# A tenth place for weights, base rows stored block by block, and edits to the routing of a two-layer graph network

## The chip, the cores and the metric

The kernel runs on one core of a Trainium2 chip, all in float32. The metric is the device time of one execution in microseconds (us); lower is better. A core has a matrix engine (TensorE, "PE" in the profile; its weight loads are "PEld"), three engines for elementwise work (VectorE "DVE", ScalarE "ACT", GpSimd "POOL"), and SyncE ("SP"), which here only issues transfers. Each engine works through its own queue in order. Transfers (DMA) can be issued from SP, ACT and POOL, and share sixteen DMA engines. "Granted clock" is the share of its full clock that TensorE was given.

## The reference, cut to what matters

Two layers run over 384 nodes of 1024 features. Each layer is graph attention, plus a mixing attention, plus a mixture of eight experts. All three parts are added to the nodes.

```python
xn = layernorm(x)
x = x + L0_gnn(xn, edges) + L0_mix(xn)      # layer 0: attention with a mask from the edges
x = x + L0_ffn(layernorm(x))                # top 2 of 8 experts: silu(a) * g, 1024 -> 352 -> 1024
xn = layernorm(x)
x = x + L1_gnn(xn, src, dst) + L1_mix(xn)   # layer 1: edge weights exp(-leaky_relu(al + ar))
x = x + L1_ffn(layernorm(x))                # top 1 of 8 experts

def L0_ffn(h):                  # the routing of layer 0
    q, k, v = split(h @ wqkv.T, 3)                       # 8 columns each
    logits = einsum(softmax(q[..., None] * k[..., None, :]), v)
    top, idx = top_k(logits, 2); scores = softmax(top)
    ...
def L1_ffn(feats):              # the routing and the experts of layer 1
    aff = feats @ centroids.T; eid = argmax(aff); alpha = sigmoid(aff[eid])
    h = layernorm(feats) * gamma[eid] + beta[eid]
    y = feats + relu(h @ w1[eid] + b1[eid]) @ w2[eid] + b2[eid]
    return alpha * y + (1 - alpha) * feats               # feats + alpha * (relu(..) @ w2 + b2)
```

## The kernel before, in words

The nodes lie in `x` as three blocks of 128 rows (index `nb`). A block is turned to "features by nodes" with eight 128x128 transposes on TensorE (`to_t`, L211): the first four are copied out of PSUM by VectorE, the others by ScalarE. `norm_on_both` (L200) normalises the first half of a block on VectorE and the second on ScalarE.

**Weights.** Every weight is a load of up to 2 MB issued by SP into a "place" of 16 KB per partition (`load_w`, L117). `ring` (L101) is a list of pools: `next_w` (L103) takes the first entry and puts it at the end, so places are used in turn. A place is free once the matmuls that read its last weight are done. There are nine places in the end: three in `wpool`, one `w_top` (L609), two `w_more` (L730), and three `w_last` (L1158), which become usable when layer 1's middle tiles are closed (`mid.close()`, L1156).

**Order.** A planner (the Tile framework) orders each engine's queue beforehand by program order and its own estimate of what is ready. An engine then waits at the head of its queue, whatever stands behind. `tc.issue_after(i)` keeps instructions behind `i` on the engine of `i`. `held` (L301) makes a transfer wait until another instruction, or the transfer it issues, is done. A pool opened in memory that earlier pools have used waits for the release of them all; with `reuse_waits="tile"` each tile waits only for the tiles it overlaps.

**Layer 0's routing** (L753 to L799). For each block, `to_router` multiplies by `wqkv`, takes the statistics and normalises, and `ready(AF.Exp, ..)` reads one element through ScalarE to bring its table in. `to_places` (L767) runs `route_block` (L351: some twenty small VectorE steps around one Exp, and again a `ready`), ranks the nodes with small matmuls (`place_both`, L383), and scatters the rows to their expert's places in DRAM (`xg0`). `to_first` (L773) gathers the rows of expert 0 by a matmul with one-hot columns into the PSUM tiles `first`. `sums` (L787) adds up the centroids' rows by eight matmuls with a matrix of ones, `csum` is its copy; `too_many` (L341) counts whether an expert got more than its places.

**Layer 0's experts** (`experts0_sorted`, L891). Expert 0 uses `keep["xe0"]`; the others load 128 rows from `xg0` (L905) and transpose them (L910), then `hidden_of` (L914), `by_feature`, and the second matmuls (L972). Results go to DRAM, and nodes gather their two rows back (`take`, L994; the last half as `take_back`, L988).

**Layer 1** (`layer1`, L1021). Block by block: gather (`take_back`), add, normalise, transpose (L1054), multiply by `w_gnn` in two halves (L1058). Then keys, the graph part, values, queries, and `w_fc` (`project`, L1161). `to_router` (L1190) mixes a block (`mix_norm`, which is the last reader of `gamma`), takes the affinities, and makes both the experts' input `xb` and the base rows in `x` (`add_normed`, L187: feats plus the residual). `to_places` scatters `xb` to `xg`, and `info` (gate and node number) to `ig`.

**Layer 1's experts** (`experts1_sorted`, L1336). Pairs of experts share one 128-row tile. For each pair: `rows_of` (transposes and `scaled`), `hidden_of` (L1371), `by_feature` (transposes, ReLU, `hT`), `give` (L1394: second matmuls L1402, times the gate L1405, then a scatter that adds to `out` in DRAM). Biases are gathered for each node (L1412), added to the base rows (L1421), and these are stored by SP (L1423) before the first scatter may add to them.

Of the kernel before, what the change touches and what calls it, by code (L numbers as in the profile page):

```python
# [10 lines left out]
F32 = mybir.dt.float32  # L11
# [6 lines left out]
P = 128  # L18
# [27 lines left out]
def gps_two_layers(ctx: ExitStack, tc: tile.TileContext, d, out: bass.AP):  # L46
# [153 lines left out]
    def norm_on_both(dst, src, mean, rinv):  # L200

        off = small.tile([P, 1], F32, tag="off", name="off")
        ve.tensor_scalar(off, mean, rinv, -1.0, op0=OP.mult, op1=OP.mult)
        first = ve.tensor_scalar(dst[:, :HB], src[:, :HB], mean, rinv, op0=OP.subtract, op1=OP.mult)
        ac.activation(dst[:, HB:D], src[:, HB:D], AF.Identity, bias=off, scale=rinv)
        return off, first
# [134 lines left out]
    def too_many(pool, tag, oh, cap):  # L341
        ps = pool.tile([P, HB], F32, tag=tag, name="total")
        for b in range(NB):
            mm(ps[:, :X], lhsT=ones_q, rhs=oh[:, b, :], start=b == 0, stop=b == NB - 1)
        most = small.tile([P, 1], F32, tag="pl_m", name="pl_m")
        ve.tensor_reduce(most, ps[:, :X], AX.X, OP.max)
# [4 lines left out]
    def route_block(ps, sums, off, rinv, apart):  # L351
# [6 lines left out]
        qk = small.tile([P, X, X], F32, tag="r_qk", name="r_qk", bufs=1)  # L358
# [5 lines left out]
        ready(AF.Sqrt, qk[:, 0, 0:1])  # L364
# [3 lines left out]
        ve.tensor_tensor(qk, qk, qkv[:, 2, None, :].to_broadcast([P, X, X]), OP.mult)  # L368
        logit = small.tile([P, X], F32, tag="r_l", name="r_l")
        ve.tensor_reduce(logit, qk, AX.X, OP.add)  # L370
# [45 lines left out]
    with ExitStack() as layer:  # L416
# [6 lines left out]
        with tc.tile_pool(name="edges", bufs=1) as ed, tc.tile_pool(name="hot", bufs=2) as hot, \  # L423
# [17 lines left out]
            for kc in range(KC):  # L441
                mm(ps[:, :3 * X], lhsT=ones_q, rhs=wr[:, kc, :], start=kc == 0, stop=kc == KC - 1)
# [6 lines left out]
            with tc.issue_after(copied[0].ins):  # L449
                ve.tensor_copy(wsum, ps[:, :3 * X])  # L450
# [283 lines left out]
        def row(cols, name, dtype=F32):  # L734
# [3 lines left out]
                "slot": row([NB], "slot4", I32), "own_e": row([NB], "own_e4", I32), "info": row([NB, 2], "info4"),  # L738
# [4 lines left out]
        with tc.tile_pool(name="ps_m0", bufs=4, space=PSUM) as pm, \  # L743
# [11 lines left out]
            def to_router(nb):  # L755
# [7 lines left out]
                off, _ = norm_on_both(xn[:, nb, :], x[:, nb, :], mean, rinv)  # L763
# [3 lines left out]
            def to_places(nb):  # L767
                oh = route_block(*queries[nb], share[:, 1, nb:nb + 1])
# [4 lines left out]
            def to_first(nb):  # L773
                for kc in range(KC):
                    mm(first[kc // 4][:, kc % 4, :], lhsT=xn[:, nb, kc * P:(kc + 1) * P], rhs=own0[:, nb, :],
                       start=nb == 0 and kc % 4 == 0, stop=nb == NB - 1 and kc % 4 == 3)
# [11 lines left out]
            for kc in range(KC):  # L788
                mm(ps[:, :X], lhsT=ones_q, rhs=cen[:, kc, :], start=kc == 0, stop=kc == KC - 1)
            to_places(NB - 1)  # L790
            to_first(NB - 1)
            ve.tensor_copy(keep["xe0"][0], first[0])
# [5 lines left out]
            ve.tensor_copy(csum, ps[:, :X])  # L798
            over0 = too_many(px, "x", both, CAP0)  # L799
# [91 lines left out]
    def experts0_sorted(keep):  # L891

        slots, share = keep["slots"], keep["share"]
        with tc.tile_pool(name="act6", bufs=1) as act, \
                tc.tile_pool(name="work6", bufs=2) as work, \
                tc.tile_pool(name="ps_h6", bufs=5, space=PSUM) as ph, \
                tc.tile_pool(name="ps_t6", bufs=3, space=PSUM) as pt:
# [88 lines left out]
            take_back(work.tile([P, D], F32, tag="xs", name="yt1").rearrange("p (a b) -> p a b", b=HB), 0)  # L986
# [34 lines left out]
    def layer1(keep=None):  # L1021


        with tc.tile_pool(name="act2", bufs=1) as act, \
                tc.tile_pool(name="work3", bufs=2) as work, \
                tc.tile_pool(name="ps_m2", bufs=4, space=PSUM) as pm, \
                tc.tile_pool(name="ps_x2", bufs=4, space=PSUM) as px:
            mid = ExitStack()
# [3 lines left out]
            xnT = act.tile([P, KC, N], F32, tag="byf", name="xnT2")  # L1032
# [3 lines left out]
            ws = [load_w(d["w_gnn"][hf]) for hf in range(2)]  # L1036
            taken, backs = None, []
# [5 lines left out]
            for nb in range(NB):  # L1043
                with ExitStack() as behind:
                    if nb:
                        behind.enter_context(tc.issue_after(normed_half.ins))
# [6 lines left out]
                    _, normed_half = norm_on_both(xn1[:, nb, :], x[:, nb, :], mean, rinv)  # L1053
                to_t(pm, xnT, xn1[:, nb, :], nb)  # L1054
# [25 lines left out]
            gamma, beta = act.tile([P, D], F32, name="gamma"), part.tile([P, D], F32, name="beta")  # L1080
# [57 lines left out]
            oT = act.tile([P, KC, N], F32, tag="byf", name="oT2")  # L1138
# [39 lines left out]
            if keep is None:  # L1178
                for nb in range(NB):
                    for hf in range(2):  # L1180
                        project(nb, hf)
                    mix_norm(nb)
                return
# [4 lines left out]
            sums, last = {}, []  # L1188

            def to_router(nb):  # L1190
                mix_norm(nb)
                xs, xb = x[:, nb, :], xn1[:, nb, :]
# [17 lines left out]
                norm_on_both(xb, xs, mean, again)  # L1210
                add_normed(xs, mean, rinv)
                sums[nb] = (ps, less, rinv)

            def to_places(nb):
# [7 lines left out]
                c = first_of(oh[:, nb, :], near, top)  # L1222
# [6 lines left out]
                ve.tensor_scalar(keep["own_e"][:, nb:nb + 1], c, -1.0, float(X), op0=OP.mult, op1=OP.add)  # L1229
                last[:] = [scatter(xg[:, :], [slot[:, nb:nb + 1]], [xb], X * CAP)]  # L1230

# [7 lines left out]
            for nb in range(1, NB):  # L1239
                project(nb, 0)  # L1240
                to_router(nb - 1)
                project(nb, 1)
                to_places(nb - 1)
# [5 lines left out]
            for g in range(2):  # L1249
                scaled(keep["xe0"][g], first[g], g, (0, 1))  # L1250
            at = [slot[:, nb:nb + 1] for nb in range(NB)]

            info = keep["info"]
            ac.activation(info[:, :, 0], most, AF.Sigmoid)
# [81 lines left out]
    def experts1_sorted(xe0):  # L1336

        with tc.tile_pool(name="act4", bufs=1) as act, \
# [6 lines left out]
            b2s = []  # L1345

            def load_rows(pair):
                xs = work.tile([P, D], F32, tag="row", name="xs4", bufs=4)
                gp.dma_start(xs, xg[pair * P:(pair + 1) * P, :])
                return xs  # L1350
# [190 lines left out]
```

## Time and profile before

| what | value |
|---|---|
| median of 3 runs | 1060.62 us (1059.91 to 1061.09) |
| the profiled execution | 1058.17 us, its span 1056.4 us |
| mean granted clock | 0.986 |
| bytes read from / written to HBM | 160.22 / 22.44 MB, 173 GB/s over the span |
| longest matmul group | L135, 512 matmuls, 165.7 us busy |
| last matmul ends | 1047.5 us |
| last output scatter issued / landed | 1048.56 / 1053.34 us |

The span is the time from the first to the last instruction; the run has 1.8 us around it. In a timeline row stand start, duration, engine, line, operation, output<-inputs, shapes, and in brackets the idle time of the engine before it and what ended it. "PE y L1402 <- SPq L1439: 2.4, 1, 2.4" reads: before the matmuls of L1402 TensorE waited 2.4 us in all, once, at most 2.4 at a time, for something released on SP's queue; a wait for a landed load shows so. In a row of windows stand the stretch, its length, busy us (and instructions), the granted clock, the share of time in which the DMA engines were busy, and GB/s. "Landing" is when a transfer's last byte has arrived.

### The profile page before, as it was taken

How to read it: one execution, taken by the hardware profiler on the slowest of the kernel's cores; microseconds unless marked ns; L12 is line 12 of the kernel's file. 1: busy time of each engine (PE TensorE's matmuls, PEld its weight loads, DVE VectorE, ACT ScalarE, POOL GpSimd, SP SyncE). 2: the span in 40 equal slices, each digit the busy share in tenths (PEclk: the TensorE clock that was granted, in tenths of full speed). 3: DMA queues.
4: the chain of work that ended last, by engine and by line, in shares of the span. 5: the costliest groups of instructions: out<-in, count | busy, mean ns of one | idle time of the engine just before them, and what ended most of it. 6: DMA issues, size and time to landing. Idle time of an engine off the chain costs nothing. (4 is left out here: it accounts for less than half of the span.)

```text
span 1056.4 us, 9529 instructions
## 1 busy us (share of the span) xinstructions
PE 1019.2 (96%) x3455; PEld 554.2 (52%) x3455; DVE 356.2 (34%) x993; ACT 270.6 (26%) x501; POOL 320.3 (30%) x277
## 2 busy tenths in 40 slices
PE   6999999999999999999998999989999999999995
PEld 5555555554455555544456666434444465656341
DVE  4580000007666766721333111043304100365321
ACT  3111111100776666621112101221212110113210
POOL 2142456566686678510001000050001100001231
PEclk9999999999999999999998999999999999998998
DMA  9939522424424342523155887969622222625994
GB/s 352 398 134 367 156 80 89 151 96 109 80 0 91 71 80 0 160 80 130 61 199 215 306 309 281 373 219 370 228 80 79 80 80 79 241 92 206 309 373 117
DMA packets 69525, 182.83 MB, mean 173 GB/s; under 512 B 21488, under 2 KB 22352, under 8 KB 69216
## 3 DMA queue, kind: packets, MB, share of 16 engines
q1 hardware_dynamic: 41072, 147.58, 38.6%
q0 software_dynamic: 25408, 29.93, 12.3%
q10 hardware_dynamic: 2992, 4.65, 1.2%
q8 instruction: 29, 0.48, 0.2%
q14 instruction: 24, 0.20, 0.1%
HBM read 160.22 MB, written 22.44 MB: 173 GB/s over the span
## 5 line engine op out<-in xcount | busy, mean ns | idle before, releaser
L482 POOL DMA_INDIRECT countd<-seen,cells x96 | 153.4, 1598 | 62.9 <-DMA countd<-seen,cells 37.7
L135 PE MATMUL mm<-xnT,w 128*128 128x384 f32 x512 | 165.7, 486 | 0.1
L135 PEld LDWEIGHTS mm<-xnT,w 128*128 128x128 f32 x512 | 97.1, 190 | 67.7 <-DVE xnT L219 0.4
L668 PE MATMUL mm<-xnT,w 128*128 128x384 f32 x384 | 132.4, 493 | 0.0
L482 POOL DMA_INDIRECT lastd<-typ,cells x96 | 96.7, 1007 | 108.4 <-DMA lastd<-typ,cells 70.9
L668 PEld LDWEIGHTS mm<-xnT,w 128*128 128x128 f32 x384 | 70.5, 190 | 56.4 <-issue 13.4
L716 PE MATMUL mm<-w,t 128*128 128x512 f32 x192 | 84.3, 595 | 0.8 <-DVE x L404 0.8
L147 PE MATMUL mm<-w,xnT 128*128 128x512 f32 x192 | 82.8, 592 | 0.0
L135 PE MATMUL mm<-t,w 128*128 128x384 f32 x256 | 82.7, 486 | 0.0
L919 PE MATMUL h<-w,xeT 128*128 128x352 f32 x224 | 68.5, 462 | 0.7 <-DVE xeT L911 0.4
L135 PEld LDWEIGHTS mm<-t,w 128*128 128x128 f32 x256 | 48.6, 190 | 33.9
L147 PEld LDWEIGHTS mm<-w,xnT 128*128 128x128 f32 x192 | 36.3, 190 | 45.5 <-issue 45.5
L716 PEld LDWEIGHTS mm<-w,t 128*128 128x128 f32 x192 | 35.9, 190 | 44.1 <-issue 42.2
L588 DVE TENSOR_TENSOR kind<-last 128x1152 f32<-128x1152 f32 x1 | 1.4, 1359 | 165.6 <-DMA last<-lastd 165.6
L919 PEld LDWEIGHTS h<-w,xeT 128*128 128x128 f32 x224 | 41.8, 190 | 23.8 <-DVE xeT L911 2.2
L294 POOL DMA_INDIRECT xg<-xn,slot x3 | 4.0, 1330 | 144.6 <-DVE xn L1175 137.6
L1058 PE MATMUL mm<-w,xnT 128*128 128x512 f32 x96 | 43.9, 617 | 1.9 <-DVE xnT L219 1.9
L1164 PE MATMUL mm<-w,oT 128*128 128x512 f32 x96 | 42.6, 595 | 0.0
L972 PE MATMUL y<-w,hT 128*128 128x512 f32 (+1 forms) x96 | 41.6, 592 | 0.0
L147 PE MATMUL mm<-w,t 128*128 128x512 f32 x96 | 41.4, 592 | 0.0
L529 ACT ACTIVATE t<-mm,cols 128x384 f32<-128x384 f32 x24 | 14.0, 581 | 107.0 <-PE mm L135 107.0
L1114 POOL TENSOR_TENSOR x<-x,beta 128x1024 f32<-128x1024 f32 x3 | 7.3, 2428 | 97.5 <-DVE x L1113 97.5
(319 smaller groups left out, 1208.2 us busy)
## 6 DMA issues: line engine op xcount, KB each, us to landing
w<-in_w1s SPq DMA_DIRECT2D x16, 1408.0 KB, 6.8
w<-in_xw2s SPq DMA_DIRECT2D x8, 2048.0 KB, 16.3
w<-in_xw SPq DMA_DIRECT2D x8, 2048.0 KB, 10.6
w<-in_w2s SPq DMA_DIRECT2D x8, 1536.0 KB, 7.3
keys<-keyd POOLq DMA_DIRECT2D x4, 1536.0 KB, 13.7
xg<-blank SPq DMA_DIRECT2D x12, 512.0 KB, 11.3
xs<-xg POOLq DMA_DIRECT2D x10, 512.0 KB, 7.0
w<-in_wk SPq DMA_DIRECT2D x2, 2048.0 KB, 16.0
```

The source lines that it names most:

```text
L135: mm(ps[:, :N], lhsT=w[:, j, kc, :], rhs=rhs[:, kc, :], start=kc == 0, stop=kc == KC - 1)
L147: mm(ps, lhsT=lhs[:, kc, nb * P:(nb + 1) * P], rhs=w[:, kc, :], start=i == 0 and kc == 0, stop=i == len(pairs) - 1 and kc == KC - 1)
L294: i = gp.indirect_dma_start(rows, bass.IndirectOffsetOnAxis(ap=at, axis=0), src, None, bounds_check=n - 1, oob_is_err=False, compute_op=op)
L482: gp.indirect_dma_start(cells[:, :], bass.IndirectOffsetOnAxis(ap=at[:, i, c:c + 1], axis=0), src[:, c:c + 1], None, bounds_check=N * N + ...
L529: ac.activation(dst[:, ob, :], ps, AF.Identity, bias=cols[:, i, ob:ob + 1], scale=1.0)
L668: mm(ps[:, :N], lhsT=w[:, j, kc, :], rhs=xnT[:, kc, :], start=kc == 0, stop=kc == KC - 1)
L716: mm(pss[hf], lhsT=src[:, kc, nb * P:(nb + 1) * P], rhs=w_out[("mwo", "wo")[part]][hf][:, kc, :], start=part == 0 and kc == 0, stop=part = ...
L919: mm(ag[i][:, :F0], lhsT=xeT[kc // 4][:, kc % 4, :], rhs=w1[kc // 4][:, kc % 4, i * F0:(i + 1) * F0], start=kc == 0, stop=kc == KC - 1)
L972: mm(y, lhsT=hT[:k, e, j, :], rhs=w2[:k, e % 2 * len(K2) + j, :], start=j == 0, stop=j == len(K2) - 1)
L1058: mm(ps, lhsT=xnT[:, kc, nb * P:(nb + 1) * P], rhs=ws[hf][:, kc, :], start=kc == 0, stop=kc == KC - 1)
L1114: gp.tensor_tensor(x[:, b, :], x[:, b, :], beta, OP.add)
L1164: mm(ps, lhsT=oT[:, kc, nb * P:(nb + 1) * P], rhs=ws[hf][:, kc, :], start=kc == 0, stop=kc == KC - 1)
```

## The change

- **A tenth place.** In layer 1, `xnT`, `oT` and `gamma` move to a pool `late` of their own, 16 KB in all. It is closed when the last block is mixed, and a pool `w_end` of one place is opened and put at the end of `ring`.
- **Base rows and biases.** Each block's base rows are stored to `out` by ScalarE as soon as they exist (`store_base`). The biases are no longer gathered by node and added to the base: for each pair, the two experts' bias rows are loaded by SP, each to 64 partitions at once, multiplied by the gate, and added where the output leaves PSUM. Layer 1's expert rows are loaded into `x` instead of tiles of their own, and outputs of pairs 1 to 3 are written there too.
- **Routing.** Column sums (`sums`, `too_many`) are one wide matmul and a reduce instead of several matmuls and a copy. In layer 0 `csum` and the count stand behind the copy of `xe0`, `route_block` writes its product to a tile of its own, and the last block has no `ready(AF.Sqrt, ..)`. The pools of layer 0's experts wait by tile. In layer 1 the second `w_gnn` load is held until block 0's last gather; a block's VectorE work stands behind the copy of the block before it in `xnT`; and `add_normed` and the gate's sigmoid stand behind the second half of the normalisation on ScalarE.

```diff
@@ norm_on_both
-        ac.activation(dst[:, HB:D], src[:, HB:D], AF.Identity, bias=off, scale=rinv)
-        return off, first
+        second = ac.activation(dst[:, HB:D], src[:, HB:D], AF.Identity, bias=off, scale=rinv)
+        return off, first, second
@@ too_many
-        for b in range(NB):
-            mm(ps[:, :X], lhsT=ones_q, rhs=oh[:, b, :], start=b == 0, stop=b == NB - 1)
+        mm(ps[:, :NB * X], lhsT=ones_q, rhs=oh.rearrange("p b e -> p (b e)"), start=True, stop=True)
+        each = small.tile([P, X], F32, tag="pl_e", name="pl_e")
+        ve.tensor_reduce(each, ps[:, :NB * X].rearrange("p (b e) -> p e b", b=NB), AX.X, OP.add)
...
@@ route_block
         ac.activation(qk, qk, AF.Exp)
-        ready(AF.Sqrt, qk[:, 0, 0:1])
+        if more:
+            ready(AF.Sqrt, qk[:, 0, 0:1])
...
-        ve.tensor_tensor(qk, qk, qkv[:, 2, None, :].to_broadcast([P, X, X]), OP.mult)
+        given = act.tile([P, X, X], F32, tag="r_g", name="r_g")
+        ve.tensor_tensor(given, qk, qkv[:, 2, None, :].to_broadcast([P, X, X]), OP.mult)
         logit = small.tile([P, X], F32, tag="r_l", name="r_l")
-        ve.tensor_reduce(logit, qk, AX.X, OP.add)
+        ve.tensor_reduce(logit, given, AX.X, OP.add)
@@ start of layer 0
-            for kc in range(KC):
-                mm(ps[:, :3 * X], lhsT=ones_q, rhs=wr[:, kc, :], start=kc == 0, stop=kc == KC - 1)
+            mm(ps[:, :KC * 3 * X], lhsT=ones_q, rhs=wr.rearrange("p k c -> p (k c)"), start=True, stop=True)
...
-                ve.tensor_copy(wsum, ps[:, :3 * X])
+                ve.tensor_reduce(wsum, ps[:, :KC * 3 * X].rearrange("p (k c) -> p c k", k=KC), AX.X, OP.add)
@@ layer 0's routing
-            for kc in range(KC):
-                mm(ps[:, :X], lhsT=ones_q, rhs=cen[:, kc, :], start=kc == 0, stop=kc == KC - 1)
+            mm(ps[:, :KC * X], lhsT=ones_q, rhs=cen.rearrange("p k c -> p (k c)"), start=True, stop=True)
             to_places(NB - 1)
-            to_first(NB - 1)
-            ve.tensor_copy(keep["xe0"][0], first[0])
+            summed = to_first(NB - 1)
+            given = ve.tensor_copy(keep["xe0"][0], first[0])
...
-            ve.tensor_copy(csum, ps[:, :X])
-            over0 = too_many(px, "x", both, CAP0)
+            with tc.issue_after(given.ins):
+                ve.tensor_reduce(csum, ps[:, :KC * X].rearrange("p (k c) -> p c k", k=KC), AX.X, OP.add)
+                with tc.issue_after(summed.ins):
+                    over0 = too_many(px, "x", both, CAP0)
@@ experts0_sorted: all four pools
-        with tc.tile_pool(name="act6", bufs=1) as act, \
+        with tc.tile_pool(name="act6", bufs=1, reuse_waits="tile") as act, \
...
-            take_back(work.tile(...), 0)
+            keep["taken"] = take_back(work.tile(...), 0)
@@ layer1
+            late = ExitStack()
+            lp = late.enter_context(tc.tile_pool(name="late", bufs=1))
...
-            xnT = act.tile([P, KC, N], F32, tag="byf", name="xnT2")
+            xnT = lp.tile([P, KC, N], F32, tag="byf", name="xnT2")
...
             ws = [load_w(d["w_gnn"][hf]) for hf in range(2)]
+            if keep is not None:
+                held(loads[-1:], keep["taken"])
...
-                        behind.enter_context(tc.issue_after(normed_half.ins))
+                        behind.enter_context(tc.issue_after(turned[0].ins))
...
-                to_t(pm, xnT, xn1[:, nb, :], nb)
+                turned = to_t(pm, xnT, xn1[:, nb, :], nb)
@@ layer1: to_router, to_places
                 mix_norm(nb)
+                if nb == NB - 1:
+                    late.close()
+                    w_end = rest.enter_context(tc.tile_pool(name="w_end", bufs=1, side="right", reuse_waits="tile"))
+                    ring.append(w_end)
...
-                norm_on_both(xb, xs, mean, again)
-                add_normed(xs, mean, rinv)
+                normed_by[:] = norm_on_both(xb, xs, mean, again)[1:]
+                with tc.issue_after(normed_by[1].ins):
+                    add_normed(xs, mean, rinv)
...
-                ve.tensor_scalar(keep["own_e"][:, nb:nb + 1], c, -1.0, float(X), op0=OP.mult, op1=OP.add)
...
+            def store_base(nb):
+                ac.dma_start(out[nb * P:(nb + 1) * P, :], x[:, nb, :])
...
                 project(nb, 1)
+                store_base(nb - 1)
                 to_places(nb - 1)
...
                 scaled(keep["xe0"][g], first[g], g, (0, 1))
+            store_base(NB - 1)
...
-            ac.activation(info[:, :, 0], most, AF.Sigmoid)
+            with tc.issue_after(normed_by[1].ins):
+                ac.activation(info[:, :, 0], most, AF.Sigmoid)
@@ experts1_sorted
+            rows = [None, *(x[:, nb, :] for nb in range(NB))]
...
-                xeT = [work.tile([P, KC // 2, P], F32, tag=f"xeT{g}", name="xeT4") for g in range(2)]
+                xeT = [work.tile([P, KC // 2, P], F32, tag=f"xeT{g}", name="xeT4", bufs=1) for g in range(2)]
...
+                es = (2 * pair, 2 * pair + 1)
+                b2 = work.tile([P, D], F32, tag="b2", name="b24")
+                for r, e in enumerate(es):
+                    nc.sync.dma_start(b2[r * CAP:(r + 1) * CAP, :], d["b2"][e:e + 1, :].to_broadcast([CAP, D]))
+                w2 = [load_w(d["xw2s"][e], (F1 // P, D)) for e in es]
+                gate = inf[:, pair, 0:1]
+                with tc.issue_after(scaled_by[0].ins):
+                    ve.tensor_scalar(b2, b2, gate, None, op0=OP.mult)
...
-                    o = work.tile([P, HB], F32, tag="o", name="o4", bufs=4)
-                    ve.tensor_scalar(o, y, inf[:, pair, 0:1], None, op0=OP.mult)
+                    o = rows[pair][:, cs] if pair else work.tile([P, HB], F32, tag="o", name="o4")
+                    ve.scalar_tensor_tensor(o, y, gate, b2[:, cs], op0=OP.mult, op1=OP.add)
...
-            for nb in range(NB):
-                b2s.append(work.tile([P, D], F32, tag="row", name="b24", bufs=4))
-                gather(b2s[nb], d["b2"], keep["own_e"][:, nb:nb + 1], X)
-            xss.update({pair: load_rows(pair) for pair in (2, 3)})
+            for pair in range(1, X // 2):
+                gp.dma_start(rows[pair], xg[pair * P:(pair + 1) * P, :])
...
-                for nb in range(NB):
-                    ve.scalar_tensor_tensor(x[:, nb, :], b2s[nb], keep["info"][:, nb, 0:1], x[:, nb, :],
-                                            op0=OP.mult, op1=OP.add)
-                    nc.sync.dma_start(out[nb * P:(nb + 1) * P, :], x[:, nb, :])
```

## The prediction

> **What bounds the kernel now.** I read the page first (busy time, 40 slices), then who waited for whom on TensorE, then TensorE in windows of 3.41 us around each dip of the granted clock, then the timelines of those places and the landing of every transfer.
>
> ```profile
> PE 1019.2 (96%) x3455; PEld 554.2 (52%) x3455; DVE 356.2 (34%) x993; ACT 270.6 (26%) x501; POOL 320.3 (30%) x277
> PEclk9999999999999999999998999999999999998998
> DMA  9939522424424342523155887969622222625994
> ```
>
> TensorE is the bound: 37 us of the span are idle, and a few more are work at half clock. The list of its waits says where:
>
> ```profile
> PE sums L442 <- DVE bmv L172: 7.7, 1, 7.7
> PE mm L218 <- DVE xn L204: 3.5, 2, 3.0
> PE rank L387 <- DVE both L769: 2.5, 1, 2.5
> PE y L1402 <- SPq L1439: 2.4, 1, 2.4
> PE mm L1058 <- DVE xnT L219: 1.9, 3, 1.2
> ...
> PE h L1371 <- SPq L1439: 1.4, 1, 1.4
> ```
>
> So there are four places: the start, the end of layer 0's routing (L387), the entry of layer 1 (L218, L1058), and the last two pairs of experts (L1371, L1402), where weights arrive late. A fifth, layer 1's routing, has small waits on slots. In windows, with TensorE's busy time and its clock:
>
> ```profile
> 558.53:561.94 3.41, 0.97 (x9) 1.00 0.40 162
> 561.94:565.36 3.41, 2.83 (x12) 0.50 0.00 0
> 565.36:568.77 3.41, 2.74 (x12) 0.50 0.45 182
> 568.77:572.18 3.41, 3.41 (x7) 0.50 0.34 130
> ```
>
> After a window with 0.97 us of work the clock is halved, and it returns after the first full one. The same is seen at 708.7 (after 0.38 us) and 971.5, for 6.8 us each.
>
> **Layer 0's routing.**
>
> ```profile
> 558.64 0.17 DVE L798 COPY csum<-sums 128x8 f32<-128x8 f32 x1 [3.11 <-PE sums L789]
> 558.73 0.21 DVE L366 TENSOR_REDUCE r_s<-r_qk 128x8 f32<-128x64 f32 x1
> 562.01 0.60 PE L387 MATMUL rank<-both,later 128*128 128x8 f32 x2 [2.51 <-DVE both L769]
> 568.01 11.79 PE L919 MATMUL h<-w,xe 128*128 128x352 f32 x32 [0.68 <-ACT xe L793]
> ```
>
> The Exp that L366 needs (L363) ended at 556.40. L366 stood on VectorE behind the copy of csum, which waited for 16 small matmuls. With csum queued behind the copy of xe0, L366 starts at 556.45: 2.28 saved. The multiply at L368 today waits for ScalarE's dummy read, which ends at 558.00; with a tile of its own and no dummy for the last block that wait is gone too (otherwise the gain is 1.0). So `both` is ready at 559.7 instead of 562.0. Moving the total's reduce away saves about 0.25 before L390, so the last 16 `first` matmuls start at 560.75 instead of 563.55. TensorE's own savings here (1.85 of sums, 1.18 of totals, nearly all cut) lie in the same wait and are worth nothing.
>
> From there: 16 `first` matmuls take 1.9 at full clock. With tile-wise waits hidden_of(0) starts at once, since its first half needs only VectorE's copy: the 0.68 goes. One expert takes 9.5 at full clock (11.02 between the row loads of successive experts, less 1.5 for transposes). The clock decides: TensorE still idles 557.6 to 559.7 and works little until 560.75. [...] I follow the row: half clock for one or two windows, end at 573.9 or 575.6, against 579.63 now. What is late next is expert 1's row load: scatters, landing, load and landing took 575.79 - 564.48 = 11.3 from the slots; slots at 561.6 put it at 572.9, so a faster hidden_of(0) would be held there. Gain 4.0, 5.7 or, capped by that load, 6.6; I take 5.5. Weights don't bind: expert 1's landed at 540.4, and later ones land some 20 us before use.
>
> **Layer 1's entry.** The second w_gnn load (issued 678.81, landed 692.63) is held until block 0's last gather. The expert stores and gathers before it landed in 4 to 7 us beside it; without it the last store (3.7) should take about 2.8, so the gathers at 699.51 come some 0.9 earlier, and so does xn (708.5). The copy L219 of xnT stood at 710.79 behind block 1's accumulate and statistics although its transposes had ended near 709.5; putting block 1 behind it saves another 1.0. Block 1 then has 5.1 us of VectorE work after the copy, under 6.9 of matmuls: hidden. Against this stands the load itself: issued at about 703.5, it lands after 7.7 (the undisturbed row at 837.58) to 13.8 (its own row now), 711.2 to 717.3. TensorE needs it half a block (3.4 us at full clock) after a start at about 708.6 to 709.4, at 712 or, at half clock, near 715. Behind it on SP stand w_k and w_v, which are held until about 712 anyway. Bounds: +4.3 if the clock stays full, -3 if the load takes its present time. It is nearer to the undisturbed row (the window 701.89 to 705.30 shows a DMA share of 0.39): gain 2.3.
>
> **The end.**
>
> ```profile
> 984.00:1040.00 56.00, 51.43 (x238) 22.42 (x236) 17.14 (x37) 12.23 (x44) 10.87 (x9) 1.00 0.98 354
> ```
>
> The DMA engines are full from 984 to 1040. Of the sixteen expert weights, number the last seven E1 to H1. With the present nine places E1 waits for hidden_of(0) (issued 984.21), the next ones stand behind three base stores that wait for VectorE (992.08), and H1 goes out at 1012.12 and lands at 1040.31, the 2.41 wait. With a tenth place each takes the place of its predecessor: E1 goes when gamma is last read (964.4), F0 and F1 at 984.2, G0 and G1 at 993, H0 and H1 at 1000.4. In DMA time after 984: E1 leaves (2.1 MB, 5.2 at 405 GB/s), the stores leave (1.57 MB, 3.9), the bias gathers (about 2.8) and the two later row loads (2.6) leave; the bias rows of pairs 2 and 3 come in (1.05 MB, 2.6). About 12 us less: the last weight lands near 1028, and is needed at 1035. Both waits go: 1.40 + 2.41 = 3.8.
>
> [...]
>
> What is added: three store issues on ScalarE, 0.33 each (L979), at gaps of 5.3, 5.3 and 2.6 us before its next instruction; they cost nothing, else 0.3 each. Eight bias loads on SP, 0.37 each; the third pair's wait for pair 0's output (993.5), and F0 is unharmed even if it stands behind them, since it went out at 992 before. Four multiplies by the gate (about 1.1 each by L1421's 1.28) replace three of 1.28 on an idle VectorE; if one is queued ahead of hT (L1391) the pair's TensorE work is late by 1.1, twice at most. The output's add rides on the 0.75 of L1405. Rows loaded into x wait for the stores' landing, near 977, before use at 1000. So 3.8, bounds 1.5 and 4.2.
>
> **Start and layer 1's routing.** The sums (L442, 3.58 at the cold clock) kept the first transposes until 11.13 though xn was ready at 10.17. One matmul of 192 columns is done by 8.4: 0.9, or -0.8 if the clock's first rise slips a window. I take 0.5. Layer 1's chain loses a convert (0.15) and gains a reduce (0.17); ScalarE's table load moves off L205, but TensorE waited for the slot. I take 0, bounds -1.7 and 1.7 for the clock's window.
>
> **Sum.** 5.5 + 2.3 + 3.8 + 0.5 = 12.1, off a span of 1056.4 in a run of 1058.17; the median of the runs is 1060.62, so 1048.5.
>
> **Rivals.** (1) A wait takes the place of the one removed: the row load and a second low window leave 3 of layer 0's 5.5, a queued multiply leaves 2 of the end's 3.8, w_gnn gives nothing: 5 to 9 us, about 1053. (2) The clock stays full at both routings: 6.6 + 4.3 + 3.8 + 1 to 2, about 1044.5. For: the gaps shrink to 2.1 and 1.7. Against: 0.97 us in a window was enough. (3) Nothing comes of it, as the planner that orders each engine's queue puts another small wait in front of L366's chain: about 1060. (4) Slower: the held w_gnn load at 703.5. Loads issued at 714 landed after 14.8 to 30.0 us, beside a_bc, countd and w_k. If it lands 21 us after issue, TensorE stands still from 712 to 724.5 and the half clock costs 3.4 more: 16 lost against 9.8 gained elsewhere, about 1066. It decides from a landing later than about 718.5. Against: those loads stood behind one another, this one goes alone.
>
> **Chances.** Forecast 0.54 (1046.5 to 1051), (1) 0.18, (2) 0.10, (3) 0.06, (4) 0.12. Faster by over 0.2% (2.1 us, about what a measurement here can tell from no change): 0.82; same 0.06; slower 0.12. The range takes the first three: 1043 to 1055.5.
>
> **What would show it.** L366 right after L363, and the first L919 near 563; expert 1's transposes near 574. In layer 1 the first L1058 3 us earlier, and no wait for SP at it. No waits of L1371 and L1402 for SP; E1 issued near the last read of gamma. Wrong: a wait of L1058 for its weights, hT behind the gate's multiply, or low clock windows elsewhere.

## The result, and the profile after

The changed kernel takes 1047.63 us (median of six runs, 1042.25 to 1051.63), the kernel before 1060.56 in the same comparison: ratio 0.9874, 95% interval 0.9840 to 0.9909. Forecast: 1048.5. The profiled execution of after is its longest: 1051.63 us, span 1049.9. Before's runs lie within 3.0 us of each other, after's within 9.4; that spread turned out to be part of the answer.

From the page of after: TensorE's busy time fell from 1019.2 to 1010.6 while the span fell by 6.5, so idle time did not fall in this execution, it rose by 2.

```profile
PE 1010.6 (96%) x3419; PEld 547.5 (52%) x3419; DVE 354.1 (34%) x993; ACT 267.7 (25%) x498; POOL 316.8 (30%) x274
PEclk9999999999999999999999999999999999998998
DMA  9949522425324332623057788969622222628993
```

TensorE's waits in after (line: what it waited for: total, times, longest):

```profile
PE sums L444 <- DMA wr<-in_wqkv: 7.9, 1, 7.9
PE y L1425 <- SPq L1456: 3.6, 1, 3.6
PE mm L218 <- DVE xn L204: 2.9, 2, 2.4
PE t L914 <- DMA xs<-xg: 2.8, 1, 2.8
PE rank L390 <- DVE both L771: 2.0, 1, 2.0
PE first L1250 <- DVE slot L1242: 1.9, 2, 1.4
```

The wait of hidden_of (L1371 of before, 1.4) is gone. The wait of the last output for its weights, which the prediction removed, is there and longer: 3.6 in place of 2.4. A new one stands in layer 0: expert 1's rows, 2.8. After's timeline of layer 0's routing:

```profile
555.98 0.22 DVE L368 TENSOR_REDUCE r_s<-r_qk 128x8 f32<-128x64 f32 x1 [0.90 <-ACT r_qk L364]
...
559.08 0.39 PE L390 MATMUL rank<-both,later 128*128 128x8 f32 x2 [2.05 <-DVE both L771]
...
562.14 9.71 PE L923 MATMUL h<-w,xe 128*128 128x352 f32 x32
...
574.65 1.16 PE L914 MATMUL t<-ident,xs 128*128 128x128 f32 x8 [2.79 <-DMA xs<-xg]
```

The reduce starts 0.03 us after its Exp, hidden_of(0) runs in 9.71 us and not 11.79, and then TensorE stands still until the rows land.

**Where the time came from.** The starts of the same TensorE work in two traces cut the span into six pieces; a piece's gain is its length in before's trace minus its length in the other. e1 is a second profile of the same changed kernel, and e7, e8, e9, e12 are runs below.

| piece, from one start to the next | before, us | after | e1 | e7 | e8 | e9 | e12 |
|---|---|---|---|---|---|---|---|
| to the first projection | 16.96 | 0.45 | 0.48 | 0.71 | 0.78 | 0.87 | 0.23 |
| to expert 1's first matmul, layer 0 | 564.12 | 4.56 | 4.86 | 5.29 | 4.74 | 5.93 | 4.68 |
| to layer 1's first matmul (back) | 119.00 | -1.38 | 0.00 | 0.00 | -1.30 | 0.00 | 0.00 |
| to the first w_gnn matmul | 11.44 | 2.17 | 2.15 | 2.23 | 1.60 | 2.19 | 1.54 |
| to hidden_of(0) of layer 1 | 264.36 | 0.57 | 2.00 | 2.01 | 0.90 | 2.00 | -0.08 |
| to the end | 80.57 | 0.17 | 0.69 | 3.59 | 3.64 | 2.60 | 6.92 |
| sum | 1056.45 | 6.54 | 10.18 | 13.83 | 10.36 | 13.59 | 13.29 |

Start, layer 0 and layer 1's entry give about what was forecast (0.5, 5.5, 2.3) in nearly every column; in after and e8 1.3 to 1.4 of layer 0's gain is lost again in the piece behind it. The end (forecast 3.8) gives anything from 0.2 to 3.6 where its code is unchanged (after, e1, e7, e8), and 6.9 in e12. So the question for the experiments was the end.

### The profile page after: what moved, and what is told of

The parts are those of the page before. It is cut to its first block, busy times and chain, and to the rows that moved or that the text cites. A ratio compares the mean times of both kernels' runs of the same rounds, so it can differ in the third digit from the quotient of the medians.

```text
span 1049.9 us, 9465 instructions
## 1 busy us (share of the span) xinstructions
PE 1010.6 (96%) x3419; PEld 547.5 (52%) x3419; DVE 354.1 (34%) x993; ACT 267.7 (25%) x498; POOL 316.8 (30%) x274
## 5 line engine op out<-in xcount | busy, mean ns | idle before, releaser
L670 PEld LDWEIGHTS mm<-xnT,w 128*128 128x128 f32 x384 | 70.6, 190 | 56.3 <-issue 13.4
L1425 PE MATMUL y<-w,hT 128*64 128x512 f32 x128 | 32.6, 625 | 3.7 <-SPq L1456 3.6
```

The lines of the kernel that those rows point to most:

```text
L670: mm(ps[:, :N], lhsT=w[:, j, kc, :], rhs=xnT[:, kc, :], start=kc == 0, stop=kc == KC - 1)
L1425: mm(y[r * CAP:(r + 1) * CAP, :], lhsT=hT[:, j, r * CAP:(r + 1) * CAP], rhs=w2[r][:, j, cs], start=j == 0, stop=j == F1 // P - 1)
```

## The experiments

Each timed run has its own runs of the kernel before beside it (median 1058.5 to 1059.7). Diffs are against the changed kernel, and line numbers are those of after in all runs (in some of the others a line stands one or two earlier). In the trace's list of DMA packets, 4 KB packets in after take 160 ns in most places, but 250 to 360 ns in stretches of some 6 us, the weights' packets too; in each of the three such stretches behind the start of hidden_of(0), bias rows b2 are in flight by their place in the queue.

**e1: the changed kernel again.**

> The changed kernel as it is, again, beside the next three. Both theories of the end (below) expect 1047.6 (ratio 0.987) and, in its profile, a wait of about 3.6 us of TensorE for the last expert weights at L1425. If the wait is an accident of that one profiled execution (rival: chance), it is missing here and in the median.

Measured: 1046.23 us (1043.67 to 1050.57), ratio 0.9881 (0.9860 to 0.9902). The wait at L1425 is 2.6, with 3.4 us of half clock behind it. So the wait is no accident of one execution.

**e2: bias rows from GpSimd's queue.**

```
-  nc.sync.dma_start(b2[r * CAP:(r + 1) * CAP, :], d["b2"][e:e + 1, :].to_broadcast([CAP, D]))
+  gp.dma_start(b2[r * CAP:(r + 1) * CAP, :], d["b2"][e:e + 1, :].to_broadcast([CAP, D]))
```

> The bias rows of the experts are loaded from GpSimd's queue, not SP's; nothing else moves. Theory A (order on SP: the weights H0 and H1 stand behind bias loads that wait for an earlier pair's output): H0 and H1 go out about 11 us earlier, near 994, the 3.6 us wait and the half clock behind it go, 4 to 5 us faster than the changed kernel. Theory B (the bias loads themselves are slow: 64 reads of one 4 KB row each, which hold the DMA engines for far longer than their bytes): the DMA engines have as much to do as before, the last weight lands within 1 us of 1032, and the time is within 1.5 us of the changed kernel.

Measured: 1049.35 (1048.92 to 1052.64), ratio 0.9909 (0.9894 to 0.9923). H0 was issued at 993.50, 12 us earlier than in after (1005.28), and still the wait at L1425 is 3.0; the last weight packet starts 63.1 us after hidden_of(0), in after 62.2. Theory A, the order on SP, falls: the engines, not the queue, are what the weights wait for.

**e3: other rows through the same loads.**

```
-  d["b2"][e:e + 1, :].to_broadcast([CAP, D])
+  d["xw2s"][e][0, :CAP, :]
```

> The bias loads keep queue, order, size and waits, but each reads 64 different rows of a weight (the first 64 partitions of xw2s) in place of 64 times one bias row, so the biases that are added are wrong. Theory A (order): the wait of 3.6 us stays, time as the changed kernel within 1.5 us. Theory B (slow reads of one row): the DMA engines move about 400 GB/s in the stretches where they moved 200 to 300, the last weight lands some 5 us earlier, the wait goes, 4 to 5 us faster than the changed kernel.

Measured: 1046.61 (1043.51 to 1051.96), ratio 0.9887 (0.9866 to 0.9909), a wait of 3.8 at L1425. Theory B falls as well: 64 different rows are as slow as 64 times one row. What is left in common is the destination, 64 partitions (theory C).

**e4: no tenth place.**

```
-  w_end = rest.enter_context(tc.tile_pool(name="w_end", bufs=1, side="right", reuse_waits="tile"))
-  ring.append(w_end)
```

> The changed kernel without the tenth weight place, all else kept. By the prediction's working the tenth place moves 2.1 MB (5.2 us of DMA time) ahead of 976; both theories expect that without it the last weight lands about 5 us later, near 1037, and the time is 4 to 6 us longer than the changed kernel (about 1053). If the place is worth nothing (rival: the end is bound by the order of SP alone), the time is within 1 us.

Measured: 1052.38 (1047.59 to 1054.75), ratio 0.9931 (0.9910 to 0.9952): 6 us above e1, as expected. In its profile the end is only 1.7 longer than e1's (81.56 against 79.88), and the delay sits elsewhere than expected: a wait of 3.3 for pair 1's rows with half clock behind it, and none for the last weights. That the tenth place is needed is shown by the medians; how its 6 us come about is not. (The bias loads of the first two pairs go out from 0.5 us after hidden_of(0) on, two of the four ahead of the rows' load at 1.9; that this makes the wait was not tried.)

**e5 and e6: one load per pair, to 128 partitions; in e6 with a third place for the bias tiles as well.**

```
-  for r, e in enumerate(es):
-      nc.sync.dma_start(b2[r * CAP:(r + 1) * CAP, :], d["b2"][e:e + 1, :].to_broadcast([CAP, D]))
+  nc.sync.dma_start(b2, bass.AP(tensor=d["b2"].tensor, offset=d["b2"].offset + es[0] * D, ap=[[D, 2], [0, CAP], [1, D]]))
```

> The two bias loads of a pair (64 rows of 4 KB to 64 partitions each) become one load to all 128 partitions; the same bytes from the same two bias rows. Packets of 4 KB took 160 ns in the stretches without bias loads and 250 to 360 ns while one was in flight, also where 64 different rows were read. Theory C (the half of the partitions): a destination of 64 partitions halves what the DMA engines write; with 128 partitions the packets stay at 160 to 180 ns, each pair gains about 2.5 us of DMA time, the last weight lands about 5 us earlier, the wait for it at the end goes, 3 to 5 us faster than the changed kernel. Theory D (what is read, or SP's issues beside the weights): packets stay at 250 to 360 ns, the time is the changed kernel's within 1.5 us.

> As the run before it, and the bias tiles have three places (pair 0's output is written over its bias rows, which frees the room): pair 2's bias load goes out with pairs 0 and 1 near 970, where the DMA engines have gaps, and the last waits for pair 0's output, not pair 1's. Theories B, C and D all expect less in the full stretch: the last weight lands another 2 to 3 us earlier than in the run before, no wait for weights at the end, and 4 to 6 us faster than the changed kernel. If the wait at the end is bound by something else (rival: the places of the weights alone), it stays at 2.5 us or more.

Measured: 1090.15 (ratio 1.0299, 1.0279 to 1.0318) and 1088.14 (1.0275, 1.0256 to 1.0295): some 43 us slower than the changed kernel. The form was a mistake and tells nothing of C. In e5, in stretches where little but a bias load moves (start and length of the window, busy time of five engines, clock, DMA share, GB/s):

```profile
1003.00:1009.00 6.00, 6.00 (x28) 3.02 (x24) 2.16 (x3) 0.00 (x0) 2.06 (x2) 1.00 0.20 56
1031.00:1038.00 7.00, 0.45 (x1) 0.29 (x2) 0.75 (x1) 0.00 (x0) 0.00 (x0) 0.50 0.13 52
```

A share of 0.13 is as much as two engines of sixteen can be busy. What sets this load apart from those of e9 and e10 below, which also write 128 partitions, is the form of its source, whose outermost dimension is the two experts; by what that comes to two engines no run shows. The issues on SP in this stretch took 6 to 12 us each, and the weights came late (at L1387 TensorE waited 15.4 us for them).

**e7: csum and the count back in front of layer 0's chain.**

```
-  with tc.issue_after(given.ins):
-      ve.tensor_reduce(csum, ...)
-      with tc.issue_after(summed.ins):
-          over0 = too_many(px, "x", both, CAP0)
+  ve.tensor_reduce(csum, ...)
+  over0 = too_many(px, "x", both, CAP0)
```

> The changed kernel with the reduce of csum and the count of the places put where they stood before, in front of the chain (L368, L371), everything else of the routing changed. By the prediction's step the copy of csum blocked that chain for 2.28 us, so both comes about 2 us later (the one matmul that it waits for is shorter than the sixteen of before, so 1 to 2.3), and so do the slots and expert 1's row load: expert 1's transposes start near 576.5 in place of 574.5. Theory 1 (the order of csum is most of layer 0's gain): 1.5 to 2.5 us longer than the changed kernel. Rival (the row load and the clock set it, the order is worth little): within 0.7 us.

Measured: 1047.26 (1044.34 to 1051.17), ratio 0.9894 (0.9874 to 0.9915), no difference from e1 that these runs can show. The rank of the last block waits 2.9 for `both` and not 2.0, and starts 543.42 after the first projection (after 542.71, before 545.29). So with everything else changed the order is worth 0.7 to 0.9 at that point, and the rest of the routing changes 1.9; theory 1 falls. Later even the 0.7 disappears (expert 1's first matmul comes earlier here than in after), since row load and clock decide there.

**e8: the second w_gnn load not held.**

```
-  held(loads[-1:], keep["taken"])
```

> The changed kernel with the second w_gnn load not held. By the prediction's step the load then runs beside the last expert stores and gathers and delays them by about 0.9 us: lead on the kernel before at the first layer-1 matmul is 0.9 smaller. By the trace of the changed kernel the gathers came only about 0.4 earlier relative to TensorE's work, so the rival expects 0 to 0.4, which no median here can show; then the first L218 of layer 1 starts as long after the first back matmul as in the changed kernel (7.8 us) within 0.4.

Measured: 1045.16 (1043.68 to 1047.82), ratio 0.9866 (0.9847 to 0.9884). From back to the first w_gnn matmul it takes 9.84, after and e1 9.27 and 9.29; but e12, with the load held, takes 9.90. The 0.9 of the forecast is not shown, and a value near 0 cannot be told from 0.5.

**e9 and e10: the two missing cells.** In e9 the host lays each bias row out 64 times (`a["b2x"] = np.repeat(b2, CAP, axis=0)`), so that one load brings 128 different rows to 128 partitions; in e10 one row is read 128 times, which leaves out the second expert's biases.

```
-  (the two loads of 64 rows)
+  nc.sync.dma_start(b2, d["b2x"][pair * P:(pair + 1) * P, :])                 # e9
+  nc.sync.dma_start(b2, d["b2"][es[0]:es[0] + 1, :].to_broadcast([P, D]))     # e10
```

> The bias rows are laid out 64 times each in the input, so a pair's biases are one load of 128 different rows of 4 KB to 128 partitions, the form of the row loads of xg (which the run with a two-row source did not have: there only about two DMA engines worked, 13 packets per us). Theory C (64 partitions halve the write): packets stay near 160 ns, each pair's load costs its bytes (1.3 us) and no more, the last weight lands about 5 us earlier, no wait at L1425, 3 to 5 us faster than the changed kernel in its profile from hidden_of(0) to the end (about 76 to 77 us in place of 80). Theory D (something else slows them, for instance a new transfer beside the weights): packets at 250 us or more while it is in flight, wait at L1425 of 2 us or more.

> One load to 128 partitions that reads one bias row 128 times (so the second expert of each pair gets the first one's bias). With the run before it and the run with 64 different rows this fills the table of 64 or 128 partitions, one row or different rows. Theory C (partitions): packets near 160 ns as in the run before it. Theory B (reads of one row): 250 to 360 ns and the wait of 2 to 4 us at L1425 as in the changed kernel. Both causes at once: between them, 200 to 250 ns.

Measured: e9 1044.57 (1044.13 to 1045.16), ratio 0.9868 (0.9852 to 0.9883); e10 1043.13 (1041.69 to 1044.17), ratio 0.9854 (0.9837 to 0.9871). No wait for weights at L1425 in either. The same 40 us of each trace, from 10.5 us after hidden_of(0) of layer 1 on (columns as above; the last two are DMA share and GB/s), first after, 64 partitions from one row:

```profile
980.00:1020.00 40.00, 39.95 (x190) 18.52 (x188) 11.30 (x26) 9.61 (x34) 6.32 (x4) 1.00 1.03 316
```

e3, 64 partitions from different rows:

```profile
977.00:1017.00 40.00, 39.46 (x190) 18.89 (x192) 11.66 (x25) 10.02 (x36) 6.32 (x4) 1.00 1.04 319
```

e9, 128 partitions from different rows:

```profile
975.40:1015.40 40.00, 39.51 (x182) 18.31 (x184) 12.67 (x27) 9.78 (x34) 6.32 (x4) 0.96 0.99 358
```

e10, 128 partitions from one row:

```profile
976.60:1016.60 40.00, 39.95 (x191) 18.56 (x191) 12.89 (x28) 9.77 (x34) 7.86 (x5) 1.00 1.02 374
```

The DMA engines are busy all the time in all four, and that is the trap of the busy share: what they move differs (before moves 380 GB/s in the same 40 us). The rows split by destination, not by source. The packets of the 66 us after hidden_of(0) show it too; "engine time" is the sum of their durations over 16, and packets are those of the loads:

| | MB moved | engine time, us | 4 KB packets over 200 ns | last weight packet after hidden_of(0), us |
|---|---|---|---|---|
| before | 20.69 | 59.0 | 126 of 4736 | 63.7 |
| after | 18.24 | 59.6 | 978 of 4003 | 62.2 |
| e1 | 18.25 | 58.8 | 873 of 4006 | 61.6 |
| e7 | 18.23 | 57.6 | 756 of 3998 | 60.6 |
| e8 | 18.22 | 57.5 | 707 of 3995 | 60.6 |
| e3 | 18.24 | 59.1 | 903 of 4004 | 64.1 |
| e9 | 18.26 | 52.8 | 150 of 4008 | 53.9 |
| e10 | 18.19 | 52.9 | 274 of 3988 | 52.6 |

After moves 2.45 MB less than before and needs as much engine time for it. With 128 partitions the same bytes take 6.8 us less than in after, 6.0 less than in e1 and 4.7 less than in e7 and e8, and the last weights come 7 to 10 us earlier. What theory C expected of the packets and of the wait came true in both runs. Its 3 to 5 us did not come in e9: the end takes 77.97 us there, 1.9 less than in e1 and more than in e7 and e8 (77.0 and 76.9), and the ratios of e9 and e1 overlap. In e10 it takes 74.75. So the source is ruled out, and the form of the load at its destination is the cause; but two loads of 64 partitions became one load of 128, and no run separates the height of a load from their number.

With bias loads in flight after moved 200 and 240 GB/s in the 4 us from 996 and from 1012, and 404 in those from 1020. An estimate from that: 2.1 MB of bias rows at half of 405 GB/s (before moved 402 and 409 in the 4 us from 988 and from 992) would cost 5.2 us more, between the measured 4.7 and 6.8. The weights' packets of the same stretches are slow too: in e2, where SP's queue carries only weights, 778 of their 3072 take over 200 ns, in e12 55. So such a load slows what flies beside it; by what path is not shown.

e9 has a wait of 1.7 us for pair 1's rows (L1376), whose load goes out behind two bias loads issued 0.4 us and less before it, and 3.4 us of half clock behind that wait. The same wait is 0.3 in e1, 0.8 in e10 and 1.3 in e3, so it does not belong to the 128 partitions.

**e11: as e9 with three places.** The bias tile gets `bufs=3`, and pair 0's output is written over its bias rows.

> The load of e9 with three places for the bias tiles (pair 0's output is written over its bias rows): pair 2's load goes out near 971 and not at 985, the last one waits for pair 0's output. Theory C: no wait at L1425, as e9, within 1 us of it; the rival (the order on SP still delays the last weights) expects e9 to keep 1 us or more of wait and this one none, 1 to 2 us faster than e9.

Measured: 1046.12 (1044.29 to 1049.61), ratio 0.9886 (0.9865 to 0.9906). No wait at L1425, but e9 had none either, so there was nothing for the third place to win; with two bias loads ahead of it and a third 0.5 us behind it, pair 1's row load is waited for 2.4 us. The rival falls.

**e12: as e9, issued by GpSimd behind the row loads.**

```
-  nc.sync.dma_start(b2, d["b2x"][pair * P:(pair + 1) * P, :])
+  gp.dma_start(b2, d["b2x"][pair * P:(pair + 1) * P, :])
```

> The bias load of e9 (128 different rows to 128 partitions), issued by GpSimd behind the row loads of xg and, for pairs 2 and 3, behind the output scatters, so that pair 1's row load no longer shares the engines with two bias loads. Theory C with the rows ahead: no wait at L1425 as in e9, and the wait of 1.7 us for pair 1's rows (L1376) that e9 had and e10 had not is gone, so hidden_of(0) of layer 1 to the end takes about 75 us (e10: 74.7), not 78 (e9) or 80 (the changed kernel), and the median is 1 to 3 us under e9's 1044.57. Rival (the 1.7 us came from the clock's windows and the base store): still a wait of 1 to 2 us at L1376, median within 1 us of e9.

Measured: 1040.75 (1040.60 to 1045.46), ratio 0.9840 (0.9816 to 0.9865): the lowest median, with an interval that overlaps those of e9 and e10. Its longest waits on TensorE:

```profile
PE sums L444 <- DVE bmv L172: 8.0, 1, 8.0
PE mm L218 <- DVE xn L204: 3.1, 2, 2.6
PE rank L390 <- DVE both L771: 2.0, 1, 2.0
PE first L1250 <- DVE slot L1242: 1.9, 2, 1.4
PE mm L218 <- DVE off L203: 1.7, 1, 1.7
PE t L1399 <- DVE hs L1390: 1.1, 2, 0.6
PE rank L330 <- DVE oh L253: 0.8, 1, 0.8
```

Neither the last weights nor pair 1's rows are waited for, and from hidden_of(0) to the end it takes 73.65 us (after 80.40). So this change's end could give 6.9, which is 3.3 to 6.8 more than it gave with the loads to 64 partitions; e10, which changes only the form of the load, gives 5.8, and e9 and e11, which stand for pair 1's rows, 2.6 and 2.1. (About 1.2 of the 6.9 is clock: before's low window of 971.5 to 978.4 reaches 2.5 us past the start of hidden_of(0), e12's ends before it.) GpSimd's queue brought no gain in e2. Here the wait for pair 1's rows is gone with it, in the one profile; the medians do not separate e12 from e9 and e10.

## Why the prediction was right, and which step failed

The time was right within 0.9 us, but partly because errors of both signs cancelled: the end came short by up to 3.6 (after), and layer 1's entry with its clock gave up to 1.9 more (e7).

- **Layer 0, forecast 5.5 (4.0 to 6.6):** 4.6 to 6.2 in all profiles, minus 1.2 to 1.4 in four of them (after, e2, e4, e8), where TensorE stood for the rows; so 3.2 in after. `both` was forecast at 559.7 and came at 559.0, 0.45 of it from the earlier start. The 2.28 came as the prediction said: the reduce (L366, now L368) starts 2.33 us after its Exp ends in before and 0.03 in after. But the order of csum is not the only way to it: in e7, with the old order, it is 0.88, because the one matmul in front of csum ends 0.7 us after the Exp where the eight ended 2.2 after it. Shorter sums were counted as worth nothing; with the new order the chain does not wait for them, with the old one they bring most of the gain (1.45 of 2.30). No run has the new order with the eight matmuls, or the last block's dummy read kept. A term that was wrong is the row load: named as what would be late next at 572.9, it landed at 574.65 in after.
- **Its clock.** The prediction followed before's window from 558.53 (gaps of 2.5 and 0.5 us, 0.97 us of work, half clock behind it); full clock was its rival 2. Both happened: in after hidden_of(0) ran at full clock and ended at 571.85, TensorE then stood for the rows, and the clock fell behind that wait, which is the -1.38 of the next piece; in e1 the clock was half from 558.8 to 565.6, hidden_of(0) ended later, and TensorE did not wait. In e9 the clock begins to fall within 557.0 to 560.4 (0.99, with 1.11 us of work), TensorE does not wait for the rows, and 5.9 are gained.
- **Layer 1's entry, forecast 2.3 (-3 to 4.3):** 1.4 to 2.2 to the first w_gnn matmul, 1.5 (e12) to 4.2 (e7) with the clock of the next piece. The 0.9 for the held load is not shown (e8). TensorE did not wait for w_gnn in any profile: the slower rival did not occur.
- **The end, forecast 3.8 (1.5 to 4.2): this step failed.** The term "the bias rows of pairs 2 and 3 come in (1.05 MB, 2.6)" priced them by bytes at the full rate. With pairs 0 and 1, whose loads fall in the full stretch too, they are 2.1 MB, and beside their bytes they cost 4.7 to 6.8 us of engine time. So of "About 12 us less" 1.5 was left in after (63.7 to 62.2 from hidden_of(0)) and 3.1 in e7 and e8; with the load of e9 it is 9.8. The three base stores were counted (3.9) because they move out of the full stretch: from 932 to 948 before has a DMA share of 0.01 and issues them only from 988.8 to 991.7, and in after ScalarE issues them at 934.4, 951.05 and 969.70; no run shows what their move alone is worth. The wait of hidden_of went. The wait for the last weights (L1402, now L1425) stayed, at 1.9 to 3.6. The gain was 0.2 and 0.7 where it was 2.6 or more and the clock fell behind it, 3.6 where it was 1.9 or 2.2 (e7, e8) and the clock did not.
- **What the late weights cost** was also sized too small, 1.40 + 2.41. The list of waits counts only time in which TensorE has nothing at all. The last pair's second matmuls in before and, behind their first two, in after:

```profile
1036.11 1.93 PE L1402 MATMUL y<-w,hT 128*64 128x512 f32 x4
1040.44 7.05 PE L1402 MATMUL y<-w,hT 128*64 128x512 f32 x28 [2.41 <-SPq L1439]
1032.49 8.75 PE L1425 MATMUL y<-w,hT 128*64 128x512 f32 x30 [3.61 <-SPq L1456]
```

The two experts of a pair normally run interleaved, and all 32 matmuls take 7.3 us (e9, e10, e12). In before the first expert's four ran alone while the other's weights were missing, and the 32 took 11.4: a loss of 4.1, not 2.41. They took 13.4 in after, half clock included, and 10.0 and 10.3 in e7 and e8. The last pair's hidden_of took 9.5 in before and 7.8 in all of these: 1.7, not 1.40. With 1.2 of clock that makes 7.0, as much as e12's 6.9. In e7 and e8 only 1.1 to 1.4 of the 4.1 was won, so that their 3.6 lies near the forecast is luck.
- **The order on SP.** "F0 is unharmed even if it stands behind them" was said of one weight; H0 and H1 did stand behind bias loads, to 1005. e2 shows that this cost nothing while the engines were full.
- **Start 0.5, layer 1's routing 0:** 0.2 to 1.0 for the start; in layer 1's routing no change but that of clock windows.
- **Rivals.** Rival 1 (a wait in the place of the one removed) is what happened at the end in after, and rival 2 (the clock stays full) is what lifts the entry in e1, e7 and e9. The span of after's runs, 1042 to 1052, covers both: 0.992 to 0.993 is the mean clock of every run up to 1045 of after and e1, and 0.988 to 0.992 of those above.

## What to carry to other kernels

Do not price a new transfer by its bytes alone: 2.1 MB of bias rows took 4.7 to 6.8 us more engine time as two loads to 64 partitions for each pair (after, e1, e7, e8) than as one to 128 (e9), and a load whose source has an outermost dimension of two moved 52 to 56 GB/s (e5). When the DMA engines are full, compare GB/s at the same busy share (316 in after, 374 in e10, at shares of 1.03 and 1.02): the slow loads here had slow neighbours (778 of 3072 packets over 200 ns on the weights' queue in e2, 55 in e12), and the busy share hid it. Beside a pair of half-height loads the last 32 matmuls took 10.0 to 13.4 us here (after, e1, e7, e8), beside one load of full height 7.3, whether it read one row 128 times (e10) or rows replicated in memory (e9, e12). A wait for weights can cost more than the list of waits shows, where matmuls that normally overlap run alone before it (4.1 us against 2.41 in before). TensorE's waits of 2.0 and 2.4 us, shorter than a clock window, each had a low window behind it in one of after and e1 and none in the other, and after's six runs lie between 1042.25 and 1051.63; so compare pieces of traces before medians.

## What the runs showed of the hardware

**Which gap halves the clock.** In before and after all changes of the granted clock lie whole numbers of windows of 3.41 us apart (in after those at 575.49 and 964.61 are 114 windows apart), and for two gaps the same wait had a low window behind it in one of after and e1 and none in the other, with the edges of the windows in other places. After, around the wait of 2.05 us for `both` and around the wait for expert 1's rows:

```profile
555.02:558.43 3.41, 2.01 (x19) 1.92 (x18) 2.23 (x15) 0.91 (x3) 0.96 (x1) 1.00 1.04 420
558.43:561.84 3.41, 2.12 (x17) 2.03 (x18) 2.70 (x18) 0.21 (x1) 0.04 (x1) 1.00 0.35 141
572.08:575.49 3.41, 0.84 (x8) 0.86 (x8) 0.17 (x1) 0.00 (x0) 0.00 (x0) 1.00 1.02 410
575.49:578.90 3.41, 3.15 (x10) 1.96 (x8) 1.37 (x3) 0.74 (x2) 0.53 (x1) 0.50 1.04 404
```

An edge splits the first gap in two, both windows keep 2.0 us of work and the clock stays; 0.84 us of work let it fall. In e1 the same gap lies in one window:

```profile
555.40:558.80 3.40, 1.49 (x15) 1.40 (x13) 2.66 (x18) 0.60 (x3) 0.63 (x1) 1.00 1.02 417
558.80:562.20 3.40, 2.63 (x11) 2.54 (x12) 1.68 (x13) 0.00 (x0) 0.35 (x1) 0.50 0.17 70
```

At layer 1's entry the gap of 2.4 us left 0.99 in one window of after (the clock fell). In e1 an edge split it: 1.43 us of work were left in the window from 698.73 and 2.62 in the next, and the clock stayed. But busy time alone draws no line. In layer 1's routing the clock fell behind windows with more work, in before behind this one (columns as in the prediction):

```profile
968.13:971.54 3.41, 2.33 (x20) 1.00 0.33 133
```

There it was 2.43 in after. Most of that work is matmuls with 8 columns, where the 1.43 that kept the clock is four matmuls with 512; what the clock goes by is not shown. None of these windows was without work.

**Half-height loads.** In after 4 KB packets took 160 ns in most places and 250 to 360 ns while 64-partition loads were in flight, other transfers' packets included; in the 4 us from 996 and from 1012 the engines, busy all the time, moved 200 and 240 GB/s. In the 66 us after hidden_of(0) 978 of 4003 packets took over 200 ns in after, 150 of 4008 in e9 and 274 of 3988 in e10, with loads to 128 partitions. A load whose source has an outermost dimension of two moved 52 to 56 GB/s (e5).
